# A fp32 cross-attention block: loads, biases and the written-out order at both ends of the kernel

## The chip, the cores and the metric

The kernel runs on one core of a Trainium2 chip. Everything is fp32. The metric is the device time of one execution in microseconds (us): 1021.24 us before the change, median of 3 runs (1021.12 to 1022.81). A core has five engines with an instruction stream each: TensorE (PE: matrix products and 128x128 transposes, with its weight loads shown apart as PEld), VectorE (DVE), ScalarE (ACT), GpSimd (POOL) and SyncE (SP), which here only issues DMAs. They wait for one another by semaphores.

## The reference

The block normalises x and the context, modulates both by a scale and a shift that come from a condition vector, and lets 1024 rows of x attend to 64 rows of context in 16 heads. There are 16 batches and 512 features.

```python
def _ada_ln(x, c, W_ss, b_ss):
    mu = jnp.mean(x, axis=-1, keepdims=True)
    var = jnp.mean((x - mu) ** 2, axis=-1, keepdims=True)
    h = (x - mu) / jnp.sqrt(var + EPS)
    ss = jax.nn.silu(c) @ W_ss + b_ss
    scale, bias = jnp.split(ss, 2, axis=-1)
    return (1.0 + scale)[:, None, :] * h + bias[:, None, :]

B, Lq, H = (16, 1024, 512); Lkv = 64; nh = 16; dh = 32
xq = _ada_ln(x_q, t_vec, Wss_q, bss_q)
xkv = _ada_ln(x_kv, t_vec, Wss_kv, bss_kv)
q = (xq @ Wq + bq).reshape(B, Lq, nh, dh)
kv = (xkv @ Wkv + bkv).reshape(B, Lkv, 2, nh, dh)
k = kv[:, :, 0]
v = kv[:, :, 1]
scores = jnp.einsum('bqhd,bkhd->bhqk', q, k) / jnp.sqrt(jnp.float32(dh))
attn = jax.nn.softmax(scores, axis=-1)
out = jnp.einsum('bhqk,bkhd->bqhd', attn, v).reshape(B, Lq, H)
return x_q + (out @ Wp + bp)
```

## The kernel before, in words

The 16 x 1024 rows of x are cut into 32 blocks of 512 rows (NB = 32, two blocks a batch). The context is two groups, "A" (batches 0 to 7) and "B" (8 to 15), of 512 rows each. Every instruction stands in a hand-written program: `manual_schedule()` keeps the order of the program as the order of each engine's queue, so a call that is moved in the text moves its instructions past others on each engine that it uses, and past DMAs on SyncE's queue.

Stages of one block i, by the names that the text calls:

- `load_x(i)` (L106) brings 1 MB, `q_stats` (L327) and `q_scale` (L334) make mean and reciprocal deviation, `hidden` (L345) normalises. `turn` (L367) transposes 32x32 squares on VectorE into the tile `ht` (one buffer), and `move` (L388) brings them to the other partitions by 16 DMAs; `scale_features` (L449) modulates the result. Context group "A" and "B" go by TensorE transposes instead (`turned_features`, L399), then `modulated` (L413) on VectorE and ScalarE; block 0 by `turned_products` (L430) and `turned_scaled` (L440).
- A 512x512x512 product is seven half-size products instead of eight (`seven`, L526): `context_product` (k and v of a group), `query_product` (q of a block), `product` (L932, the projection). Each is 8 records of 128x256. They need sums of operands: `column_sums` (weights, L467), `feature_sums` (L484), `row_sums` (L920), `weight_sums` (L882), nearly all on GpSimd. `context_out`, `query_out`, `query_added` and `added` (L959) take the results from PSUM. v goes to a staging tile and from there by `value_move` (L631), 8 DMAs a half, to V_A or V_B. Below, k1 or v3 is product 1 of k, or 3 of v; p11 is projection product 1 of block 1, z2 product 2 of the last block.
- `score_products(i, z)` (L656) for the two halves z of the 64 keys, `maximum` and `copied` (L679, L688) for each pair of banks, `maxima` (L714) spreads the maximum, `subtract` (L720, GpSimd, 4.55 us a half), `weights` (L726, exponentials on ScalarE), `total` (L758, GpSimd) and `row_total` (L765, VectorE) sum them. The tile of `total(i)` is one that the scores of block i+1 are copied into. `inverse_rows` (L779) takes reciprocals and brings them through DRAM (`ltd`, then `vr`), `spread_rows` (L790) spreads them, `mix` (L815) multiplies the weights by V, and `divided` (L798) divides into the tile `ot`.
- `load_residual` brings x again, `residual` (L357) adds the projection's bias on GpSimd for block 29, `biased` (L907) copies it into PSUM for the others, and `added` adds and stores.

The way in (L985 to L1407) sets up the modulation, runs both context groups and blocks 0 to 2, all ordered by hand. The loop `for i in range(3, NB - 2)` (L1409 to L1481) then does, for block i, the scores, and around them the projection of blocks i-2 and i-1 and the queries of block i+1. The way out (L1483 to L1577) ends blocks y = 30 and z = 31.

At the very start, 36 transposes of the identity (`warm`, L985) run on TensorE while the first loads are on their way. `load_scale_shift` (L139) brings the weights of the scale and shift in two parts j of two 512-KB DMAs; `scale_shift_rows` (L253) multiplies the condition by one part, `scale_shift_taken` (L271) copies the rows from PSUM, `scale_shift` (L275) transposes them and adds the biases. The biases come as a 24x128 tile by four small DMAs from GpSimd (`load_biases`, L153), and one transpose turns them (`biases`, L236).

What sets the order of DMAs is SyncE's queue. Tiles come from pools with few buffers (x: 2, `ht`: 1, the staging tile of v: 1, shared with the weight sums), so a load or a turn can wait until a former user is done.

Of the kernel before, what the change touches and what calls it, by code (L numbers as in the profile page):

```python
# [9 lines left out]
F32 = mybir.dt.float32  # L10
AF = mybir.ActivationFunctionType
ALU = mybir.AluOpType
# [8 lines left out]
def cross_attention_block(  # L21
# [117 lines left out]
    def load_scale_shift(name, w, j):  # L139
        pool, tag = SS_HOMES[name, j]  # L140
        t = pool.tile([P, NC, H], F32, tag=tag, name=f"wss_{name}_{j}")
        for h in range(2):
            at = h * H + j * (H // 2)
            nc.sync.dma_start(
                t[:, :, h * (H // 2) : (h + 1) * (H // 2)],
                w[:, at : at + H // 2].rearrange("(c p) o -> p c o", p=P),
            )
# [59 lines left out]
    ident = const.tile([P, P], F32, name="ident")  # L207
    make_identity(nc, ident)
    load_biases()
# [7 lines left out]
    WARM = 36  # L217
# [18 lines left out]
    def biases():  # L236
        pb = bank("pb", 1)
        nc.tensor.transpose(pb[:, :NBR], brow, ident[:NBR, :NBR])
        nc.vector.tensor_copy(bias_t, pb[:, :NBR])
        ones = bias_t[:, : 4 * NC].rearrange("p (n h c) -> p n h c", n=2, h=2)[:, :, 0, :]  # L240
        nc.vector.tensor_scalar_add(ones, ones, 1.0)
# [673 lines left out]
    s1_tiles, s2_tiles = {}, {}  # L915
# [4 lines left out]
    def row_sums(i, n):  # L920
# [6 lines left out]
        else:  # L927
            s2_tiles[i] = opool.tile([P, HC, HT], F32, tag="s2", name=f"s2_{i}")
            tt(s2_tiles[i], half_rows(i, 1, 1), s1_tiles[i], ALU.subtract)  # L929
            tt(half_rows(i, 0, 1), half_rows(i, 0, 1), s2_tiles[i], ALU.subtract)  # L930

    def product(i, n):  # L932
# [5 lines left out]
            4: (lambda: half_rows(i, 0, 1), lambda: half_weights(1, 1)),  # L938
# [48 lines left out]
    load_x("B")  # L987
    q_stats("A", (0,))
    q_stats("A", (1,))
    column_sums("k", w_k_sb, w_k_sums, (2,))  # L990
    first_scale(0)
    hidden("A", (0,))
    biases()
    scale_shift_rows("kv", 0)
    hidden("A", (1,))
    scale_shift_taken("kv", 0)
    turned_features("A", 0)
    scale_shift("kv", 2 * NC, 0)
    modulated("A", 0, 0, nc.vector)
    column_sums("k", w_k_sb, w_k_sums, (0,))  # L1000
    column_sums("k", w_k_sb, w_k_sums, (1,))
    q_stats("A", (2,))
    turned_features("A", 1)
    modulated("A", 0, 0, nc.scalar)
    load_query_weights()
    q_stats("A", (3,))
    column_sums("v", w_v_sb, wv_sums, (2,))
    column_sums("v", w_v_sb, wv_sums, (0,))
    first_scale(1)
    context_product("A", "k", 1)  # L1010
    hidden("A", (3,))
    scale_shift_rows("kv", 1)
    turned_features("A", 3)
    hidden("A", (2,))
    scale_shift_taken("kv", 1)
    scale_shift("kv", 2 * NC, 1)
    context_out("A", "k", 1)
    turned_features("A", 2)
    modulated("A", 0, 1, nc.scalar)
    modulated("A", 1, 1, nc.vector)  # L1020
    modulated("A", 1, 0, nc.scalar)
    modulated("A", 1, 0, nc.vector)
    context_product("A", "v", 1)
    modulated("A", 0, 1, nc.vector)
    context_product("A", "k", 2)
    context_out("A", "v", 1)
    modulated("A", 1, 1, nc.scalar)
    feature_sums("A", nc.vector, (0,))
    context_product("A", "v", 2)
    context_out("A", "k", 2)  # L1030
    context_product("A", "k", 7)
    column_sums("v", w_v_sb, wv_sums, (1,))
    feature_sums("A", nc.vector, (1,))
    column_sums("k", w_k_sb, w_k_sums, (3,))
    context_out("A", "v", 2)
    column_sums("v", w_v_sb, wv_sums, (3,))
    feature_sums("A", nc.vector, (2,))
    load_x(1)
    q_stats(0, (0,))
    q_stats(0, (1,))  # L1040
    q_stats(0, (2,))
    context_product("A", "v", 7)
    q_stats(0, (3,))
    context_product("A", "v", 6)
    q_scale(0)
    hidden(0, (2,))
    scale_shift_rows("q", 0)
    context_out("A", "v", 6)
    hidden(0, (0,))
    hidden(0, (1,))  # L1050
    hidden(0, (3,))
    scale_shift_rows("q", 1)
    context_out("A", "k", 7)
    scale_shift_taken("q", 0, 2)
    context_product("A", "k", 6)
    scale_shift("q", 0, 0, 2)
    turned_products()
    q_stats("B", (0,))
    context_out("A", "v", 7)
    q_stats("B", (3,))  # L1060
    turned_scaled(1)
    context_out("A", "k", 6)
    q_stats("B", (1,))
    column_sums("q", w_q_sb, w_q_sums, (2,))
    turned_scaled(2)
    context_product("A", "v", 5)
    q_stats("B", (2,))
    column_sums("q", w_q_sb, w_q_sums, (0,))
    q_scale("B")
    turned_scaled(3)  # L1070
    turned_scaled(0)
    hidden("B", (0,))
    hidden("B", (1,))
    context_out("A", "v", 5)
    context_product("A", "k", 5)
    context_out("A", "k", 5)
    context_product("A", "v", 3)
    hidden("B", (3,))
    feature_sums("A", nc.vector, (3,))
    context_product("A", "k", 3)  # L1080
    context_out("A", "v", 3)
    turned_features("B", 0)
    feature_sums(0, nc.gpsimd, (0,))
    feature_sums(0, nc.gpsimd, (1,))
    q_stats(1, (0,))
    turned_features("B", 1)
    q_stats(1, (3,))
    feature_sums(0, nc.gpsimd, (2,))
    turned_features("B", 3)
    q_stats(1, (2,))  # L1090
    context_out("A", "k", 3)
    context_product("A", "k", 4)
    hidden("B", (2,))
    modulated("B", 1, 1, nc.scalar)
    column_sums("q", w_q_sb, w_q_sums, (1,))
    q_stats(1, (1,))
    turned_features("B", 2)
    modulated("B", 0, 0, nc.scalar)
    query_product(0, 1)
    modulated("B", 0, 0, nc.vector)  # L1100
    q_scale(1)
    load_x(2)
    modulated("B", 1, 1, nc.vector)
    feature_sums(0, nc.gpsimd, (3,))
    modulated("B", 0, 1, nc.scalar)
    context_out("A", "k", 4)
    value_move("A", 0)
    hidden(1, (0,))
    query_seed(0)
    hidden(1, (1,))  # L1110
    modulated("B", 0, 1, nc.vector)
    feature_sums("B", nc.gpsimd, (0,))
    feature_sums("B", nc.gpsimd, (1,))
    context_product("B", "k", 1)
    hidden(1, (2,))
    load_x(3)
    column_sums("q", w_q_sb, w_q_sums, (3,))
    turn(1, (0,))
    modulated("B", 1, 0, nc.vector)
    context_product("A", "v", 4)  # L1120
    hidden(1, (3,))
    turn(1, (1,))
    query_product(0, 6)
    context_out("A", "v", 4)
    load_projection_bias()
    turn(1, (2,))
    turn(1, (3,))
    move(1, two=True)
    feature_sums("B", nc.gpsimd, (2,))
    q_stats(2, (0,))  # L1130
    modulated("B", 1, 0, nc.scalar)
    q_stats(2, (2,))
    context_out("B", "k", 1)
    query_product(0, 2)
    context_product("B", "k", 2)
    q_stats(2, (3,))
    query_out(0, 2)
    query_out(0, 6)
    context_out("B", "k", 2)
    query_product(0, 7)  # L1140
# [477 lines left out]
```

## Time and profile before

| | |
|---|---|
| median of 3 runs | 1021.24 us |
| the profiled execution: its own time | 1021.5 us |
| its span | 1019.7 us |
| mean granted TensorE clock | 0.999 |
| busy: TensorE, VectorE, GpSimd, ScalarE | 99%, 85%, 80%, 63% |
| way in: setup up to the first product of block 0 | 9.8 to 46.3 us |
| scores of block 0, 1, 2 (first half of keys) | 68.8, 93.8, 121.7 us |
| first projection product of block 1 | 145.7 us |
| way out: scores of block 30 | 943.3 us |
| last product begins | 1013.9 us |

Times in views of the trace count from the start of the span. A row of the timeline gives start, length, engine, line, operation, the tile written and the tiles read, shapes and the number of merged instructions; in square brackets stands how long the engine had been idle and what ended that. The matrix records are counted twice a call, since an fp32 call makes two. PE's, DVE's, ACT's and POOL's rows are work; SP's are issues of DMAs, whose data land later. Busy shares are averages over stages.

### The profile page before, as it was taken

The numbers are of one execution on the slowest core, as the hardware profiler recorded it, in microseconds if no ns is written. First come the engines' busy times: TensorE is split into PE (matmuls) and PEld (weight loads), VectorE is DVE, ScalarE is ACT, GpSimd is POOL, SyncE is SP. The second block draws the span as 40 slices with busy tenths as digits, with TensorE's granted clock in tenths as the row PEclk, the third lists the DMA queues.
The fourth block names the chain that finished last, engine by engine and source line by source line (L and its number), as shares of the span: only waits on it lengthen the run. The fifth ranks groups of instructions, "written<-read, shape, count | busy, mean of one in ns | idle before, by whom it ended". The sixth has DMA issues, their size and how long they took to land.

```text
span 1019.7 us, 21267 instructions
## 1 busy us (share of the span) xinstructions
PE 1006.6 (99%) x8101; PEld 767.5 (75%) x8101; DVE 862.8 (85%) x1181; ACT 638.3 (63%) x1025; POOL 811.4 (80%) x522
## 2 busy tenths in 40 slices
PE   8999999999999999999999999999999999999998
PEld 6887777777777777787777777877777777777746
DVE  6777888888898888888988888889888888876794
ACT  3777756666666666666666666667666666665530
POOL 3658898887988888889888888898888888987861
PEclk9999999999999999999999999999999999999999
DMA  9565544444445444444554444444544444335122
GB/s 314 194 177 160 148 155 134 138 144 156 156 157 167 147 130 144 127 156 148 162 167 128 127 158 133 154 155 160 167 134 127 123 155 156 117 121 167 45 86 86
DMA packets 112165, 149.82 MB, mean 147 GB/s; under 512 B 34072, under 2 KB 45360, under 8 KB 112064
## 3 DMA queue, kind: packets, MB, share of 16 engines
q1 hardware_dynamic: 111680, 147.94, 45.4%
q8 instruction: 64, 1.05, 0.4%
q0 software_dynamic: 384, 0.54, 0.2%
q14 instruction: 37, 0.30, 0.1%
HBM read 79.21 MB, written 34.60 MB: 112 GB/s over the span
## 4 chain that ended last, share of the span: by engine, by line
PE 74%; POOL 3%; DVE 3%; SPq 2%; DMA 2%; ACT 2%; issue 1%; DVEq 0%; POOLq 0%; ACTq 0%
PE pp L950 32%; PE pq L544 31%; PE ps L663 6%; PE po L831 5%; SPq L394 2%; POOL s L722 1%; DMA x<-in_x_dram 1%; ACT s L728 1%; POOL xt_sums L503 1%; DVE m L680 1%; DVE mb L709 0%; DVE l L733 0%; DMA xt<-ht 0%; ACT xt L452 0%; ACT qt L583 0%
## 5 line engine op out<-in xcount | busy, mean ns | idle before, releaser
L722 POOL TENSOR_TENSOR s<-s,mb 128x2048 f32<-128x2048 f32 x64 | 290.3, 4562 | 128.2 <-DVE mb L709 128.2
L689 ACT COPY s<-ps 128x1024 f32<-128x1024 f32 x128 | 129.5, 1013 | 106.9 <-DVE m L680 63.0
L680 DVE TRANSPOSE_TENSOR_REDUCE m<-ps 128x32 f32<-128x1024 f32 x128 | 151.3, 1217 | 32.6 <-PE ps L663 32.6
L950 PE MATMUL pp<-w_p_sb,ot 128*128 128x256 f32 x744 | 171.3, 379 | 1.4 <-DVE ot L811 0.9
L974 DVE TENSOR_TENSOR r<-pp,r 128x512 f32<-128x512 f32 x210 | 136.6, 671 | 34.3 <-PE pp L950 29.1
L950 PEld LDWEIGHTS pp<-w_p_sb,ot 128*128 128x128 f32 x744 | 141.1, 190 | 22.1 <-ACT qt L583 1.3
L583 ACT ACTIVATE qt<-pq,bias_t 128x256 f32<-128x256 f32 x256 | 105.8, 465 | 76.6 <-PE pq L544 76.4
L728 ACT ACTIVATE s<-s 128x2048 f32<-128x2048 f32 x64 | 122.4, 1912 | 40.6 <-POOL s L722 40.6
L762 POOL TENSOR_TENSOR sum<-s,s 128x2048 f32<-128x2048 f32 x31 | 140.8, 4543 | 4.3 <-ACT s L728 4.3
L950 PEld LDWEIGHTS pp<-WT,s 128*128 128x128 f32 x496 | 89.4, 189 | 58.2 <-issue 28.5
L950 PE MATMUL pp<-WT,s 128*128 128x256 f32 x496 | 123.2, 391 | 0.2 <-POOL s L929 0.2
L544 PE MATMUL pq<-xt_sums,w_q_sums 128*128 128x256 f32 x512 | 123.3, 384 | 0.0
L544 PE MATMUL pq<-xt,w_q_sb 128*128 128x256 f32 x512 | 121.5, 380 | 0.0
L544 PEld LDWEIGHTS pq<-xt_sums,w_q_sums 128*128 128x128 f32 x512 | 95.0, 190 | 34.5 <-issue 22.6
L544 PE MATMUL pq<-xt,w_q_sums 128*128 128x256 f32 x512 | 120.9, 379 | 0.0
L950 PE MATMUL pp<-WT,ot 128*128 128x256 f32 x496 | 117.5, 380 | 0.7 <-POOL ot L926 0.6
L544 PEld LDWEIGHTS pq<-xt,w_q_sb 128*128 128x128 f32 x512 | 96.8, 190 | 17.1 <-issue 2.5
L544 PEld LDWEIGHTS pq<-xt,w_q_sums 128*128 128x128 f32 x512 | 97.3, 190 | 13.2
L950 PEld LDWEIGHTS pp<-WT,ot 128*128 128x128 f32 x496 | 93.9, 190 | 15.1 <-POOL ot L926 1.0
L452 ACT ACTIVATE xt<-xt,ss_q 128x512 f32<-128x512 f32 x124 | 94.2, 809 | 8.5 <-DMA ltd<-lt 5.6
L341 ACT ACTIVATE x<-x,rstdq 128x512 f32<-128x512 f32 x128 | 97.3, 809 | 2.1 <-POOL rstdq L316 2.1
L503 POOL TENSOR_TENSOR xt_sums<-xt 128x512 f32<-128x512 f32 x64 | 81.7, 1277 | 10.4 <-ACT xt L452 7.5
(173 smaller groups left out, 1489.7 us busy)
## 6 DMA issues: line engine op xcount, KB each, us to landing
x<-in_x_dram SPq DMA_DIRECT2D x32, 1024.0 KB, 5.7
r<-in_x_dram SPq DMA_DIRECT2D x32, 1024.0 KB, 5.1
xt<-ht SPq DMA_DIRECT2D x488, 64.0 KB, 2.0
out_dram<-r SPq DMA_DIRECT2D x60, 512.0 KB, 3.7
wss_kv<-in_L_xcond_Wss_kv_dram SPq DMA_DIRECT2D x4, 512.0 KB, 8.0
wss_q<-in_L_xcond_Wss_q_dram SPq DMA_DIRECT2D x4, 512.0 KB, 10.4
vr<-ltd SPq DMA_DIRECT2D x128, 8.0 KB, 1.6
out_dram<-r SPq DMA_DIRECT2D x7, 256.0 KB, 2.1
```

What stands on the lines that cost most here:

```text
L341: nc.scalar.activation(dst, src, AF.Identity, bias=rstd[:, 1, j : j + 1], scale=rstd[:, 0, j : j + 1])
L452: nc.scalar.activation(xt[:, :, c, :], xt[:, :, c, :], AF.Identity, scale=ss["q"][:, c, b : b + 1], bias=ss["q"][:, NC + c, b : b + 1],)
L503: eng.tensor_tensor(dst, a, b, ALU.subtract)
L544: nc.tensor.matmul(out_, lhsT=lhsT, rhs=rhs, start=new and m == 0 and c == 0, stop=c == HC - 1, skip_group_check=True,)
L583: nc.scalar.activation(dst, src, AF.Identity, bias=bq_t[:, o : o + 1])
L680: nc.vector.tensor_reduce(m_tiles[i][:, z, 2 * e : 2 * e + 2, :], s_banks[i, z][e].rearrange("p r (j a) -> p r j a", a=32), AX.X, ALU.max, ...
L689: nc.scalar.copy(s_tiles[i, z][:, 2 * e : 2 * e + 2, :], s_banks[i, z][e])
L722: eng.tensor_tensor(s_tiles[i, z], s_tiles[i, z], mb_tiles[i], ALU.subtract)
L728: nc.scalar.activation(p, p, AF.Exp, scale=SCALE)
L762: nc.gpsimd.tensor_tensor(t, s_tiles[i, 0], s_tiles[i, 1], ALU.add)
L950: nc.tensor.matmul(acc[k][:, t * HO : (t + 1) * HO], lhsT=rows[:, c, t * P : (t + 1) * P], rhs=cols[:, c, :], start=n == 2 and t == 0 and ...
L974: nc.vector.tensor_add(r, a, r)
```

## The change: loads, biases, way in and way out

The changed kernel does five things; the loop's text is the same.

1. Part 0 of the context's scale and shift weights comes in four DMAs of 128 features (256 KB) instead of two of 512 KB.
2. The biases come by SyncE in two parts: the 8 rows of the context's scale and shift first, the other 16 later, each with a transpose of its own.
3. The other loads are no longer all issued at the top: they stand between the steps. `WARM` is 34 instead of 36, and nine transposes of the identity (`keep_busy`) stand between the setup's steps.
4. The steps of the way in stand in a new order: both row products of the context's modulation and all four transposes of group "A" come before its first product, and the calls of groups "A", "B" and blocks 0 to 2 are mixed anew.
5. In the way out the query products of the last block come earlier, `residual(y - 1)` moves from its head to behind `mix(y - 1)`, `mix(z)` moves up, the products of y and z have another order, and the sum s4 of the last block goes into a tile of its own.

```diff
     def load_scale_shift(name, w, j):
         pool, tag = SS_HOMES[name, j]
         t = pool.tile([P, NC, H], F32, tag=tag, name=f"wss_{name}_{j}")
+        half = H // 2
+        if (name, j) == ("kv", 0):
+            rows = w.rearrange("(c p) (h o) -> p c h o", p=P, h=2)
+            for c in range(NC):
+                nc.sync.dma_start(
+                    t[:, c, :].rearrange("p (h o) -> p h o", h=2), rows[:, c, :, :half]
+                )
+        else:
...
-    brow = early_tile(NBR, P)
-    def load_biases():
+    brow = [early_tile(2 * NC, P), early_tile(NBR - 2 * NC, P)]
+    BIASES = (((b_ss_kv, 2 * NC),), ((b_ss_q, 2 * NC), (b_q, NC), (b_kv[0:H], NC)))
+    def load_biases(k):
         at = 0
-        for src, n in ((b_ss_q, 2 * NC), (b_ss_kv, 2 * NC), (b_q, NC), (b_kv[0:H], NC)):
-            nc.gpsimd.dma_start(brow[at : at + n, :], src.rearrange("(r f) -> r f", f=P))
+        for src, n in BIASES[k]:
+            nc.sync.dma_start(brow[k][at : at + n, :], src.rearrange("(r f) -> r f", f=P))
             at += n
...
     load_first(0)
     load_first(1)
     load_scale_shift("kv", w_ss_kv, 0)
-    load_context_weights(0, 0)
-    load_first(2)
-    load_first(3)
-    load_scale_shift("kv", w_ss_kv, 1)
-    load_context_weights(1, 0)
-    load_context_weights(0, 1)
-    load_context_weights(1, 1)
-    load_value_bias()
-    load_x(0)
-    load_scale_shift("q", w_ss_q, 0)
-    load_scale_shift("q", w_ss_q, 1)
...
-    WARM = 36
+    WARM = 34
...
+            s4 = half_rows(i, 0, 1)
+            if i == NB - 1:
+                s4 = rpool.tile([P, HPC * TB], F32, tag="spread", name="s4")
+                s4 = s4[:, : HC * HT].rearrange("p (c n) -> p c n", c=HC)
+            s4_tiles[i] = s4
+            tt(s4, half_rows(i, 0, 1), s2_tiles[i], ALU.subtract)
...
-    load_x("B")
+    idle = bank("idle", 0)
+
+    def keep_busy(n):
+        for _ in range(n):
+            nc.tensor.transpose(idle[:, :P], ident, ident)
+
```

The way in of the changed kernel, from behind the warm-up to its first product (lines that do not bear on the setup are left out):

```python
    q_stats("A", (0,))
    q_stats("A", (1,))
    load_first(2)
    first_scale(0)
    load_biases(0)
    hidden("A", (0,))
    load_first(3)
    load_scale_shift("kv", w_ss_kv, 1)
    scale_shift_rows("kv", 0)
    keep_busy(2)
    biases(0)
    hidden("A", (1,))
    q_stats("A", (2,))
    load_context_weights(0, 0)
    scale_shift_taken("kv", 0)
    load_biases(1)
    load_context_weights(1, 0)
    q_stats("A", (3,))
    turned_features("A", 0)
    turned_features("A", 1)
    load_context_weights(0, 1)
    load_context_weights(1, 1)
    keep_busy(3)
    scale_shift("kv", 2 * NC, 0)
    modulated("A", 0, 0, nc.vector)
    first_scale(1)
    keep_busy(4)
    scale_shift_rows("kv", 1)
    modulated("A", 0, 0, nc.scalar)
    ...
    turned_features("A", 2)
    ...
    turned_features("A", 3)
    ...
    scale_shift("kv", 2 * NC, 1)
    ...
    biases(1)
    context_product("A", "k", 1)
```

Further on, between the scores of block 1 and the first projection product of block 1 (changed kernel, the calls that the prediction speaks of):

```python
    total(0)
    ...
    move(3)
    ...
    score_products(1, 0)
    row_total(0)
    copied(1, 0, 0)
    maximum(1, 0, 1)
    context_product("B", "v", 5)
    maximum(1, 0, 0)
    inverse_rows(0)
    context_product("B", "v", 7)
    ...
    context_out("B", "v", 7)
    copied(1, 0, 1)
    score_products(1, 1)
    maximum(1, 1, 0)
    maximum(1, 1, 1)
    maxima(1)
    query_product(2, 1)
    ...
    context_out("B", "v", 5)
    ...
    mix(0)
    q_stats(5, (0,))
    turn(4, (0,))
    turn(4, (1,))
    context_product("B", "v", 3)
    context_out("B", "v", 3)
    ...
    value_move("B", 0)
    ...
    value_move("B", 1)
    ...
    load_x(6)
    ...
    move(4)
    ...
    inverse_rows(1)
    ...
    spread_rows(1)
    added(0, 4)
    turn(5, (1,))
    added(0, 3)
    ...
    divided(1)
    ...
    product(1, 1)
```

`value_move("A", 1)` stands in the changed kernel behind `move(2)` and before `load_x(5)` and `move(3)`; before, it stood ahead of `load_x(4)` and `move(2)`.

The way out from the last block's scores on, changed kernel:

```python
    scores(z, 0, crossed=True)
    total(y)
    mix(y - 1, apart=False, ks=(2, 3, 1, 0))
    residual(y - 1)
    divided(y - 1)
    scores(z, 1)
    row_total(y)
    project(y - 1, 0)
    inverse_rows(y)
    maxima(z)
    project(y - 1, 1)
    project(y - 1, 2, later=True)
    subtract(z)
    load_residual(y)
    spread_rows(y)
    projected(y - 1, 2)
    weights(z, 0)
    mix(y)
    weights(z, 1)
    project(y - 1, 3, later=True)
    divided(y)
    row_sums(y, 0)
    product(y, 1)
    sums(z, 0)
    product(y, 2)
    added(y, 1)
    sums(z, 1)
    halves_total(z)
    mix(z)
    inverse_rows(z)
    projected(y - 1, 3)
    row_sums(y, 1)
    product(y, 6)
    added(y, 2)
    product(y, 7)
    added(y, 6)
    product(y, 5)
    added(y, 7)
    biased(z, 2)
    product(y, 4)
    added(y, 5)
    product(y, 3)
    spread_rows(z)
    divided(z)
    row_sums(z, 0)
    product(z, 1)
    biased(z, 3)
    added(y, 3)
    added(y, 4)
    row_sums(z, 1)
    product(z, 2)
    added(z, 1)
    ...
```

More of the change, by code (lines that the diff above doesn't have):

```diff
@@ L1032, in cross_attention_block @@
[L1032 to L1038, printed above, removed]
+    hidden("A", (3,))
+    turned_features("A", 2)
+    column_sums("k", w_k_sb, w_k_sums, (0,))
+    turned_features("A", 3)
+    column_sums("v", w_v_sb, wv_sums, (0,))
+    modulated("A", 0, 1, nc.scalar)
+    scale_shift("kv", 2 * NC, 1)
@@ L1065, in cross_attention_block @@
[L1065 to L1082, printed above, removed]
@@ L1119, in cross_attention_block @@
+    query_seed(0)
     modulated("B", 1, 0, nc.vector)
     context_product("A", "v", 4)
-    hidden(1, (3,))
-    turn(1, (1,))
-    query_product(0, 6)
[L1124 to L1130, printed above, removed]
+    context_out("A", "v", 3)
+    hidden(1, (0,))
+    modulated("B", 0, 0, nc.vector)
+    hidden(1, (1,))
+    turn(1, (0,))
+    load_x(3)
+    hidden(1, (2,))
@@ L1172, in cross_attention_block @@
+    turn(2, (3,))
+    copied(0, 0, 1)
+    scale_features(1, (2,))
+    maximum(0, 0, 1)
+    context_product("B", "k", 4)
+    copied(0, 0, 0)
+    load_x(4)
+    q_scale(3)
+    score_products(0, 1)
+    scale_features(1, (3,))
+    query_product(1, 1)
+    context_out("B", "k", 5)
+    context_out("B", "k", 4)
+    context_product("B", "k", 3)
+    maximum(0, 1, 0)
+    maximum(0, 1, 1)
+    maxima(0)
+    move(2)
+    hidden(3, (0,))
+    query_seed(1)
+    context_out("B", "k", 3)
     feature_sums(1, nc.gpsimd, (0,))
-    context_product("B", "k", 5)
@@ L1226, in cross_attention_block @@
[L1226 to L1238 removed]
+    context_out("B", "v", 6)
+    query_out(1, 3)
+    scale_features(2, (1,))
+    score_products(1, 0)
+    row_total(0)
+    copied(1, 0, 0)
+    feature_sums(2, nc.gpsimd, (0,))
+    maximum(1, 0, 1)
+    context_product("B", "v", 5)
```

678 lines of the change are left out of this document (343 added, 335 removed).

## The prediction

> **What bounds the kernel now.** I read the page first, for the engine that is never idle, and then the busy time by stretch, to see in which stage that engine waits.
>
> ```profile
> span 1019.7 us, 21267 instructions
> ...
> PE 1006.6 (99%) x8101; PEld 767.5 (75%) x8101; DVE 862.8 (85%) x1181; ACT 638.3 (63%) x1025; POOL 811.4 (80%) x522
> ```
>
> ```profile
> 9.70:35.90 26.20, 24.14 (x231) 19.03 (x231) 19.63 (x53) 11.87 (x33) 12.38 (x13) 1.00 0.96 324
> 145.70:943.30 797.60, 797.41 (x6522) 609.83 (x6522) 697.06 (x909) 519.22 (x807) 666.85 (x406) 1.00 0.46 146
> 943.30:1014.00 70.70, 68.56 (x546) 45.88 (x546) 52.41 (x56) 21.83 (x25) 43.66 (x22) 1.00 0.19 67
> ```
>
> In the second table the columns are the stretch, its length, then the busy time of TensorE, its weight loads, VectorE, ScalarE and GpSimd, the granted clock, the DMA share and GB/s. TensorE is the bound. In the loop (145.7 to 943.3) it is busy 797.41 of 797.60 us, and the loop's text is the same in both kernels: nothing is to be had there. The change can only win TensorE's idle time outside it: 2.06 us in the first stretch (26.20 less 24.14), 2.14 us in the way out (70.70 less 68.56), and what the middle of the way in holds. So the question is how many of these few microseconds go, and whether they are paid again further on. A difference of 0.2%, 2.04 us, is about what a measurement of this kernel can tell from no change.
>
> **The change part by part: setup.** These are TensorE's instructions in the first 36 us (start, length, line, operation, count, and in brackets the wait before it), and the DMA queue's order.
>
> ```profile
> 3.13 6.59 PE L986 MATMUL warm<-ident 128*128 128x128 f32 x36
> ...
> 9.95 1.08 PE L260 MATMUL ps_kv<-wss_kv,early 128*32 128x128 f32 x32
> ...
> 13.00 2.15 PE L544 MATMUL pk_A<-xk_A,w_k_sb 128*128 128x256 f32 x8 [0.79 <-ACT xk_A L426]
> 15.09 1.60 PE L260 MATMUL ps_kv<-wss_kv,early 128*32 128x128 f32 x32
> ...
> 18.23 1.89 PE L544 MATMUL pv_A<-w_v_sb,xk_A 128*128 128x256 f32 x8
> ...
> 29.78 1.71 PE L260 MATMUL ss_q<-wss_q,early 128*32 128x128 f32 x56
> ...
> 34.31 1.72 PE L435 MATMUL pxt<-ident,x 128*128 128x128 f32 x14 [0.42 <-DVE ss_q L288]
> ```
>
> ```profile
> 3.15 0.51 SPq L167 DMA_DIRECT2D w_k_sb<-in_L_xcond_Wkv_dram  x1
> ```
>
> First weights in four loads: the last byte comes through the same pipe, so the last quarter lands no earlier than the second half did; only three quarters of the row products can run before it. The rows start right behind the warm-up (9.95 against 3.13 + 6.59 = 9.72, with one small transpose between). Two dummies fewer are 2 x 6.59/36 = 0.37 us. Bounds: 0 (the last quarter decides) to 1.08 us (all rows hidden); I take 0.5 for the first row. It matters little, since k1 no longer follows it directly.
>
> In a sentence apart: the Trainium skill, "DMA: Bandwidth & Descriptors", section "Rules for kernel authors", asks for at least 1 MiB in one DMA, and so speaks against quarter loads of 256 KB; the trace moves 324 GB/s over the first stretch with loads of 256 to 1024 KB, and I estimate that by the page's fixed cost of about 2 us a DMA, paid in a row, two more loads would put the first rows 4 us later, while by the trace, where issued loads overlap, they cost their issue (0.51 us each) and nothing behind that.
>
> Biases on the SyncE queue: two or three more issues of about 0.5 us (the row at 3.15) stand in front of later loads. They hide as long as the pipe is full, which it is (share 0.96). Without that cover they cost some 1.5 us once. The split adds a transpose and three short VectorE operations in gaps; I set them at nothing (bounds 0 to 0.5).
>
> Order of the setup: k1 stood at 13.00, between the two row groups; now both groups, all transposes and nine dummies come first. The second row group took 1.60 instead of 1.08 us: its second half waited till about 15.6. In the changed queue the 512-KB half of w_k (issued at 3.15) stands behind that load, which gains 0.52 MB / 324 GB/s = 1.6 us, so it lands near 14.0. From the end of that wait to v1 at 18.23 passed 2.6 us; so k1 comes between 14.0 + 2.6 = 16.6 and 17.8, since all four context tiles must now be modulated before; I take 17.2. It is 4.2 us later, but then nothing stands between the products. With 1.72 us for a product (1012.20 to 1013.92, quoted below), nine of them are 15.5, the 64 records of the query rows 1.71 x 64/56 = 1.95, the sixteen transposes of block 0 1.72 x 16/14 + 0.42 = 2.4, small ones 0.2: the end of that group comes at 17.2 + 20.0 = 37.2, with one product more than the 36.03 of before (34.31 + 1.72) had. So 35.5 against 36.0: a gain of 0.5, bounds -0.1 and +1.1.
>
> **The middle.** Here is what stands between the scores of block 1 and the first projection product of block 1, whose time fixes the loop's start, as the same four products follow it in both kernels.
>
> ```profile
> 96.28 2.27 DVE L767 TRANSPOSE_TENSOR_REDUCE lt<-sum 128x64 f32<-128x2048 f32 x1
> ...
> 100.90 2.38 DVE L680 TRANSPOSE_TENSOR_REDUCE m<-ps 128x32 f32<-128x1024 f32 x2 [0.18 <-PE ps L663]
> ...
> 106.65 0.66 DVE L624 TENSOR_TENSOR stage_B<-pv_B,b_v_sb 128x512 f32<-128x512 f32 x1
> ```
>
> ```profile
> 99.70 2.17 PE L663 MATMUL ps<-qt,K_A 32*32 32x512 f32 x32 [1.13 <-ACT s L689]
> ```
>
> ```profile
> 107.34 13.28 SPq L636 DMA_DIRECT2D V_B<-stage_B  x16
> ...
> 121.36 11.84 SPq L394 DMA_DIRECT2D xt<-ht  x16
> ```
>
> ```profile
> 139.73 2.31 DVE L793 STREAM_TRANSPOSE vb<-vr 128x2048 f32<-128x2048 f32 x1 [0.31 <-DMA vr<-ltd]
> ...
> 143.14 1.28 DVE L372 STREAM_TRANSPOSE ht<-x 128x512 f32<-128x512 f32 x2
> 144.34 2.32 DVE L811 TENSOR_TENSOR ot<-po,vb 128x1024 f32<-128x1024 f32 x2
> ```
>
> ```profile
> 145.68 1.53 PE L950 MATMUL pp<-w_p_sb,ot 128*128 128x256 f32 x6 [0.90 <-DVE ot L811]
> ```
>
> The second scores waited 1.13 us for copies that could not write before the row total (96.28 + 2.27) had read their tile. The row total is now put ahead of both maxima, its sum ahead of other GpSimd work: I take that wait as gone. So TensorE is about 0.5 + 1.1 us ahead at 100.
>
> But p11 waits for the division, that for the spread, that for rows through DRAM, and those stand on SyncE behind 32 transfers, V_B (13.28 us) and move(4) (11.84 us), which start only when v3 is staged (106.65 + 0.66 = 107.31, then 107.34). That queue is the lock. In the changed order v3 stands behind more of VectorE: the maxima start at 100.90 - 1.6 = 99.3; from there to v3 passed 5.75 us (106.65 - 100.90); v5's addition (0.66, as v3's) and two turns of block 4 (1.28) are put in front. That is 99.3 + 5.75 + 1.94 = 107.0, with some drains 107.3: V_B starts at 107.6 to 108.0, 0.3 to 0.7 later in spite of the earlier scores. Behind the spread one turn fewer (0.64) stands before the division. So p11 comes at 145.7 + 0.5 - 0.64: 0.2 us earlier, and TensorE, ahead by 1.6, waits for it longer than the 0.90 of now. Bounds: -1.6 (the lock moves as early as the scores do) and +0.6. What the head won is mostly lost again here.
>
> **The way out.** TensorE, ScalarE, VectorE and GpSimd there:
>
> ```profile
> 990.83 1.99 PE L950 MATMUL pp<-WT,ot 128*128 128x256 f32 x8 [0.60 <-POOL ot L926]
> ...
> 994.97 1.97 PE L950 MATMUL pp<-w_p_sb,ot 128*128 128x256 f32 x8 [0.42 <-DVE r L974]
> ...
> 998.59 2.35 PE L831 MATMUL po<-s,V_B 32*32 32x512 f32 x64
> ...
> 1002.99 3.72 PE L950 MATMUL pp<-w_p_sb,ot 128*128 128x256 f32 x16
> ...
> 1012.20 1.89 PE L950 MATMUL pp<-w_p_sb,ot 128*128 128x256 f32 x8
> 1013.92 1.89 PE L950 MATMUL pp<-WT,ot 128*128 128x256 f32 x8
> ```
>
> ```profile
> 988.59 0.59 ACT L913 COPY pp<-b_p_sb 128x512 f32<-128x512 f32 x1 [2.95 <-DVE r L871]
> ```
>
> ```profile
> 993.72 0.55 DVE L782 RECIPROCAL lt<-lt 128x64 f32<-128x64 f32 x1
> ...
> 999.30 2.30 DVE L793 STREAM_TRANSPOSE vb<-vr 128x2048 f32<-128x2048 f32 x1
> 1001.71 2.35 DVE L811 TENSOR_TENSOR ot<-po,vb 128x1024 f32<-128x1024 f32 x2
> ```
>
> ```profile
> 949.50 4.97 POOL L359 TENSOR_TENSOR r<-r,b_p_sb 128x512 f32<-128x512 f32 x4
> ...
> 979.13 9.07 POOL L722 TENSOR_TENSOR s<-s,mb 128x2048 f32<-128x2048 f32 x2 [8.64 <-DVE mb L709]
> ```
>
> mix(z), 2.35 us at 998.59, moves up behind the first two projection products and fills the 0.60 and 0.42 us waits: 1.0 at most. That counts only if the last block's products can start earlier. Its division hangs on the reciprocal at 993.72; the bias copy (0.59) ahead of the last exponentials goes, and with it about 0.75 us of that chain: division at 1001.0 to 1003.3. Then the adds of p3 and p4 stand on VectorE, 0.65 each: z2 cannot take its bank before 1003.3 + 1.3 = 1004.6. Before, z1 and z2 are the sixteen records at 1002.99, so z2 started at 1002.99 + 1.72 = 1004.7. So z1 gains 0.75, z2 nothing, and those behind it the short wait for row sums, which the earlier division removes. I take 0.4 (bounds 1.0 and -0.4, if an add slips one more place). The last block's s4 in its own tile costs no instruction. The residual (4.97 us on GpSimd) moves into the 8.64 us in which it waits before 979.13: nothing; without that cover it would push the last chain by up to 5.
>
> **Sum:** -0.2 (all ahead of the loop) - 0.4 (way out) = -0.6 on the profiled 1021.5, 1020.9. That run lies 0.26 above the median of 1021.24, so the forecast for the median is 1020.6.
>
> **The rivals.** *A lock that opens.* If v3 is staged as early as the scores allow, the 1.6 us won by then reach the loop, and the way out gives its 1.0: 1021.24 - 2.6 = 1018.6; with the rest of the idle time of the first stretch, up to 1 us more, 1017.6. For it: p11 hangs on one VectorE order, where half a microsecond decides. Against: the two turns and v5 are written ahead of v3.
>
> *The queue of moves shuts later* (the slower one). V_A's second half, 5.18 us, now stands behind move(2) and ahead of move(3).
>
> ```profile
> 62.66 5.18 SPq L636 DMA_DIRECT2D V_A<-stage_A  x8
> ...
> 72.38 11.98 SPq L394 DMA_DIRECT2D xt<-ht  x16
> ...
> 92.20 10.02 SPq L394 DMA_DIRECT2D xt<-ht  x16
> ```
>
> ```profile
> xt<-ht SPq DMA_DIRECT2D x488, 64.0 KB, 2.0
> ```
>
> Block 4's turns write the tile that move(3) reads, and v3 is behind them. If move(3) starts 5.18 later than now, it is issued by 107.4 and landed at 109.4; turns 1.28, v3 0.66: V_B at 111.4, 4.0 late, less 0.64 and 0.4: 1021.24 + 3.0 = 1024.2. It decides from a landing past 106 on. Against it: move(2) is over at 84.4, V_A then at 89.6, and move(3) would be issued from there on, ahead of its 92.20 of now, landing at 104.
>
> *It doesn't do what it says:* the last quarter lands with the old second half, the waits change place, 1021.2.
>
> *A cold TensorE.* The view of line 986 shows the weight loads of the warm-up, minimum, median and maximum:
>
> ```profile
> L986 PEld LDWEIGHTS warm<-ident x36: 139/230/230, 3.1 to 9.3; 128*128 128x128 f32 x36
> ```
>
> More than half of them ran at 230 ns, at least 18 x 6.59/36 = 3.3 us, before the rate of 139. If the thin work up to 17.2 lets that state come back, the same 3.3 us at 139/230 of the rate lose 3.3 x 0.4 = 1.3 us: 1021.24 - 0.6 + 1.3 = 1021.9. The nine dummies speak against it. The Trainium skill, "TensorE: Matmul & The Clock Gate", Part 1, has this rule: the clock halves after an idle window of about 3.4 us; by its figure the loss would be an estimated 1.7 us, and the trace agrees as to the start (230 to 139), while the granted clock stays at 1.00 in its rows.
>
> **How the numbers follow.** Forecast 0.42, lock open 0.32, moves late 0.17, no effect 0.04, cold 0.05. The second is faster by over 0.2%, the third slower by over 0.2%, the others (0.51) within. The forecast's own range, from the bounds above, is 1019.2 to 1022.2. The range for 8 in 10 takes in the open lock down to 1017.4 and the late moves up to 1023.4.
>
> **What would show it.** Right: first rows near 9.5, k1 near 17, products without gaps to 37, no wait before the second scores of block 1, V_B issued from about 107.8, p11 near 145.5 with a wait of over 2 us ahead of it; in the way out mix(z) near 990, division near 1001, the last product near 1013.4 less the head's 0.2. Wrong: V_B before 106.5 or p11 before 144.5 (lock open), move(3) after 95 (moves late), products of over 2.3 us around 17 to 21 (cold), or a wait of GpSimd's subtraction of the last block past 979.

## The result and the profile after

The changed kernel takes 1019.43 us (median of 8, 1018.54 to 1021.49), the kernel before, in the same session, 1022.06 us (median of 8, 1020.81 to 1023.13). The ratio is 0.9977, interval 0.9967 to 0.9986: about 2.35 us faster (1.4 to 3.4). The forecast was 0.6 us faster, which it called no measurable change; its range for 8 in 10 (1017.4 to 1023.4) held the time.

The one profiled execution of the changed kernel took 1021.49 us, the slowest of its eight, and its span, 1019.7 us, equals that of before. So the spans say nothing; the stages do. The loop has the same text in both kernels, but in these two profiles it lasts 790.7 us after (153.09 to 943.80) and 788.8 us before (154.49 to 943.29). The view of the waits from 144 to 943 us shows what one execution of it can meet (engine, line, what it waited for, total, times, longest):

```profile
ACT xt L455 <- DMA xt<-ht: 3.8, 4, 1.9
...
PE pq L547 <- ACT qt L586: 1.4, 2, 0.7
```

Twice TensorE stood 0.7 us: a query product waited for ScalarE, and ScalarE had waited up to 1.9 us for a landing of the moves. Over all fourteen profiles of this study the loop lasts between 788.2 and 790.7 us. What the change does must therefore be read ahead of 154 us and behind 943 us.

TensorE in the setup and at the first scores of block 0, changed kernel (same columns as in the prediction):

```profile
9.36 1.08 PE L263 MATMUL ps_kv<-wss_kv,early 128*32 128x128 f32 x32
...
14.21 1.07 PE L263 MATMUL ps_kv<-wss_kv,early 128*32 128x128 f32 x28 [0.68 <-DMA wss_kv<-in_L_xcond_Wss_kv_dram]
15.78 1.09 PE L410 MATMUL pxk_A<-ident,x_A 128*128 128x128 f32 x8 [0.51 <-DVE x_A L354]
...
17.07 2.00 PE L547 MATMUL pk_A<-xk_A,w_k_sb 128*128 128x256 f32 x8
...
24.31 2.00 PE L547 MATMUL pk_A<-xk_sums_A,w_k_sums 128*128 128x256 f32 x8
26.62 1.96 PE L547 MATMUL pk_A<-xk_sums_A,w_k_sums 128*128 128x256 f32 x8 [0.32 <-DVE xk_sums_A L506]
...
36.30 2.17 PE L438 MATMUL pxt<-ident,x 128*128 128x128 f32 x16
```

The second row weights land near 14.2 (forecast 14.0) and k1 starts at 17.07 (forecast 17.2). From there to the end of block 0's transposes at 38.31 (36.30 + 2.01, the next product's start) pass 21.24 us, where the forecast summed 20.0. With nine products done instead of eight that is 38.31 - 1.72 = 36.6, against 35.87 before (the start of the product behind block 0's transposes): in these two profiles the setup is 0.7 us behind, not 0.5 ahead.

The middle, TensorE, then SyncE, then VectorE:

```profile
67.78 1.14 PE L666 MATMUL ps<-qt,K_A 32*32 32x512 f32 x32
...
93.40 1.61 PE L666 MATMUL ps<-qt,K_A 32*32 32x512 f32 x32 [0.37 <-ACT qt L586]
...
99.02 1.30 PE L666 MATMUL ps<-qt,K_A 32*32 32x512 f32 x32 [0.36 <-ACT s L692]
...
100.25 1.99 PE L547 MATMUL pq<-xt,w_q_sb 128*128 128x256 f32 x8
...
123.65 1.14 PE L666 MATMUL ps<-qt,K_A 32*32 32x512 f32 x32
...
128.37 1.14 PE L666 MATMUL ps<-qt,K_A 32*32 32x512 f32 x32
...
133.09 2.35 PE L834 MATMUL po<-s,V_A 32*32 32x512 f32 x64
...
144.11 1.89 PE L958 MATMUL pp<-w_p_sb,ot 128*128 128x256 f32 x8
...
153.09 1.14 PE L666 MATMUL ps<-qt,K_A 32*32 32x512 f32 x32
```

```profile
108.93 10.37 SPq L639 DMA_DIRECT2D V_B<-stage_B  x16
```

```profile
138.63 2.27 DVE L796 STREAM_TRANSPOSE vb<-vr 128x2048 f32<-128x2048 f32 x1
...
142.59 2.34 DVE L814 TENSOR_TENSOR ot<-po,vb 128x1024 f32<-128x1024 f32 x2
```

The first projection product of block 1 (p11) has no wait any more and comes at 144.11 instead of 145.68, although V_B begins 1.6 us later than before. From the first scores of block 0 to the first of block 3, TensorE needs 153.09 - 67.78 = 85.31 us, with one product more in it (at 67.78 one fewer had been done): 83.6 against 85.7 before (154.49 - 68.80). Two more profiles with the old way in, among the experiments below, have 85.26, so this gain is 1.7 to 2.1 us. TensorE before:

```profile
68.80 1.14 PE L663 MATMUL ps<-qt,K_A 32*32 32x512 f32 x32
...
101.80 1.99 PE L544 MATMUL pv_B<-w_v_sb,xk_sums_B 128*128 128x256 f32 x8
...
121.74 1.14 PE L663 MATMUL ps<-qt,K_A 32*32 32x512 f32 x32
...
126.99 1.30 PE L663 MATMUL ps<-qt,K_A 32*32 32x512 f32 x32
...
131.87 2.35 PE L831 MATMUL po<-s,V_A 32*32 32x512 f32 x64
...
154.49 1.14 PE L663 MATMUL ps<-qt,K_A 32*32 32x512 f32 x32
```

The gain has three places. Up to the end of block 1's scores it is 0.5 us (100.25 - 67.78 = 32.47 against 101.80 - 68.80 = 33.00). From there to block 2's scores the new order has two more products, and with 1.73 us for each there is no difference. From block 2's scores to the mix of block 1 it is 0.7 us (9.44 against 10.13, with as many products). From that mix to block 3's scores, past p11, the new order has one product fewer: 20.00 + 1.73 = 21.73 us stand against 22.62 here and 22.2 in the two other profiles of the old way in, a gain of 0.5 to 0.9.

The way out, TensorE and VectorE:

```profile
943.80 1.14 PE L666 MATMUL ps<-qt,K_B 32*32 32x512 f32 x32
...
990.66 2.35 PE L834 MATMUL po<-s,V_B 32*32 32x512 f32 x64
...
1002.74 1.97 PE L958 MATMUL pp<-w_p_sb,ot 128*128 128x256 f32 x8 [0.90 <-DVE ot L814]
1005.07 1.97 PE L958 MATMUL pp<-w_p_sb,ot 128*128 128x256 f32 x8 [0.36 <-DVE r L982]
...
1013.78 1.89 PE L958 MATMUL pp<-WT,ot 128*128 128x256 f32 x8
```

```profile
1001.37 2.35 DVE L814 TENSOR_TENSOR ot<-po,vb 128x1024 f32<-128x1024 f32 x2
```

From the scores of block 30 to the last product: 69.98 us, before 70.63 (1013.92 - 943.29). The waits of 0.60 and 0.42 us are gone and two new ones, 0.90 (for the division) and 0.36 (for an add), stand ahead of z1 and z2. Together: 1.40 us ahead of the loop and 0.65 behind it, 2.05 of the 2.35 measured.

### The profile page after: what moved, and what is told of

Its sections match the earlier page's. It is cut to its first block, busy times and chain, and to the rows that moved or that the text cites. A ratio compares the mean times of both kernels' runs of the same rounds, so it can differ in the third digit from the quotient of the medians.

```text
span 1019.7 us, 21289 instructions
## 1 busy us (share of the span) xinstructions
PE 1007.1 (99%) x8109; PEld 770.6 (76%) x8109; DVE 864.3 (85%) x1184; ACT 637.6 (63%) x1025; POOL 808.1 (79%) x518
## 4 chain that ended last, share of the span: by engine, by line
PE 88%; DVE 3%; POOL 3%; DMA 2%; ACT 1%; SPq 1%; issue 1%; DVEq 0%; POOLq 0%; ACTq 0%
PE pp L958 35%; PE pq L547 35%; PE po L834 7%; PE ps L666 6%; POOL s L725 2%; PE pp L861 1%; PE pk_A L547 1%; PE pv_A L547 1%; PE pk_B L547 1%; SPq L397 1%; ACT s L731 1%; DVE m L683 1%; DMA wss_kv<-in_L_xcond_Wss_kv_dram 1%; DMA x<-in_x_dram 1%; DVE mb L712 0%
## 5 line engine op out<-in xcount | busy, mean ns | idle before, releaser
L301 DVE BATCH_NORM_STATS2 bs<-x 128x6 f32<-128x512 f32 x128 | 87.0, 680 | 0.3 <-DMA x<-in_x_dram 0.3
```

The source lines that it names most:

```text
L301: nc.vector.bn_stats(bs, r)
```

## The experiments

The theories: *queue* (SyncE's V_B, which before stood 2.9 us in its middle for v4's addition, held p11), *VectorE's order*, and *TensorE's order*. Times are compared with the kernel before; positions come from one profile of each kernel.

**Each end alone.** The kernel before with the new way out, and the changed kernel with the old way out.

> The kernel before with the changed way out alone (with the last block's s4 tile). If the two ends add up, the way in and the loop are as before: first projection product of block 1 (p11) at 145.7 us, and from the first scores of block 30 to the begin of the last product 70.0 instead of 70.6 us, so the time falls by about 0.5 us (ratio 0.9995). A rival says that the changed way out needs the changed way in to pay: then no difference in that stretch.

> The changed kernel with the way out of before. If the two ends add up: p11 at 144.1 instead of 145.7, the stretch of the way out 70.6 us as before, time lower by about 1.6 us (ratio 0.9984). The rival, that the loop gives the head's gain back (in the one profile of the changed kernel the scores of block 30 came at 943.8, later than before), says that the ratio is 1.000 within its interval.

New way out alone: ratio 0.9989 (0.9981 to 0.9998), its stretch 1012.79 - 942.81 = 69.98 us. New way in alone: 0.9982 (0.9973 to 0.9991), p11 at 144.01, way out 1012.67 - 942.03 = 70.64. The two ends add up to 0.9971, the whole change has 0.9977 (0.9967 to 0.9986). The rivals, that one needs the other or that the loop eats the gain, fall.

**The queue: its pause closed in the old kernel, and v4 put back late in the new one.** Before, SyncE's transfers to V_B stand still in their middle till VectorE has added v4 (SyncE, then VectorE):

```profile
110.97 1.90 SPq L636 DMA_DIRECT2D V_B<-stage_B  x3
...
115.53 1.87 SPq L636 DMA_DIRECT2D V_B<-stage_B  x3
```

```profile
114.84 0.66 DVE L629 TENSOR_TENSOR stage_B<-pv_B,stage_B 128x512 f32<-128x512 f32 x1
```

From 112.87 to 115.53 nothing is issued; the view of the queue's waits counts 2.9 us.

```diff
     spread_rows(0)
+    context_out("B", "v", 4)
     turn(4, (0,))
...
     product(0, 1)
-    context_out("B", "v", 4)
     query_added(2, 5)
```

> The kernel before, with one VectorE instruction moved: the addition of v4 into the staging tile stands right behind the spread of block 0 instead of behind its division. Queue theory (SyncE stood 2.9 us in the middle of V_B's sixteen transfers for this addition): V_B is issued without a gap in about 10.4 us instead of 13.3, the spread of block 1 comes up to 2.5 us earlier, p11 loses its wait of 0.9 and starts at 144.8, time lower by 0.9 us (ratio 0.9991). Rival (the gain is TensorE's own new order and the scores' shorter waits): V_B's gap closes, p11 moves by less than 0.2.

> The changed kernel, with the addition of v4 put back behind the division and the first projection product of block 0, as before. Queue theory: V_B's second half waits until about 115.4, the sixteen end near 120.6 instead of 119.3, p11 has a wait again and comes 0.8 to 1.2 us later than 144.1, time about 1 us over the changed kernel's (ratio to before near 0.9987 instead of 0.9977). Rival (TensorE's order): p11 stays within 0.2 of 144.1.

With v4 early in the kernel before, SyncE and TensorE:

```profile
107.38 11.22 SPq L636 DMA_DIRECT2D V_B<-stage_B  x16
```

```profile
145.28 1.97 PE L950 MATMUL pp<-w_p_sb,ot 128*128 128x256 f32 x8 [0.47 <-DVE ot L811]
```

The gap in V_B is closed (11.22 instead of 13.28 us), but p11 still waits 0.47; the ratio is 0.9994 (0.9985 to 1.0004). The first experiment's way in, unaltered from before and with 12.44 us for V_B, also shows 0.47 there, and both need 85.26 us from block 0's scores to block 3's: closing the gap won nothing. Of the 0.90 in the profile of before, some 0.4 go with the late landing ahead of its spread (the wait of 0.31 at 139.73 in the prediction's rows), which the other two profiles do not have. In the changed kernel with v4 late (reverse edit), the addition still came at 113.66, as the division ahead of it was early, and V_B took 10.94 instead of 10.37 us. The pause was hardly there again, so this run does not test the queue. Its p11 stood at 143.72 with the first scores at 67.38: 76.34 us between them, as in the changed kernel (144.11 - 67.78 = 76.33). The ratio is 0.9972 (0.9960 to 0.9984). The expected 0.8 to 1.2 us did not come. That the queue is not what the change gained rests on the run in the old kernel.

**Three moves of VectorE's new order, in the old kernel.**

```diff
-    maximum(1, 0, 1)
     row_total(0)
+    maximum(1, 0, 1)
...
     spread_rows(0)
+    context_out("B", "v", 4)
...
-    q_stats(6, (2,))
     turn(5, (0,))
...
-    turn(5, (2,))
     divided(1)
+    q_stats(6, (2,))
+    turn(5, (2,))
```

> The kernel before with three moves on VectorE alone in the middle of the way in: the row total of block 0 ahead of both maxima, v4's addition right behind the spread of block 0, and one statistic and one turn put behind the division of block 1. If VectorE's order is what sets the middle (the scores of block 1 and the first projection product of block 1, p11), the scores' 1.13 us wait falls below 0.4, p11's 0.90 goes, p11 starts near 144.0 and the time falls by about 1.6 us (ratio 0.9984, as the whole changed way in). Rival: the new order on TensorE is needed as well, and p11 stays later than 144.9 (ratio 0.9992 or more).

```profile
100.53 2.17 PE L663 MATMUL ps<-qt,K_A 32*32 32x512 f32 x32 [1.53 <-ACT s L689]
...
145.43 1.89 PE L950 MATMUL pp<-w_p_sb,ot 128*128 128x256 f32 x8
```

The row total ahead of both maxima made the scores' wait longer, 1.53 instead of 1.13 us, since the maxima, and the copies behind them, now came after it. In the changed kernel the first copy stands ahead of the maxima too (`copied(1, 0, 0)` in the listing ahead of the prediction), and the copies start at 96.89, 0.1 us behind the row total; here they started at 99.46. p11's wait went: from the mix of block 1 to block 3's scores TensorE took 154.29 - 132.69 = 21.60 us, against 22.2 with v4 early alone, so the statistic and the turn behind the division are worth 0.6 us there. The row total lost 0.4 (102.62 - 69.22 = 33.40 to the end of block 1's scores, against 33.00). Ratio 0.9998 (0.9988 to 1.0007): the three moves together gain nothing that the times show. They are not VectorE's whole new order, which was not run alone.

**TensorE's order around the scores of block 2.** First the old kernel with one query product moved ahead of them (and, not shown in the cut, the statistic and the turn put behind the division as above), then the changed kernel with the same product put back.

```diff
+    query_product(3, 1)
     score_products(2, 0)
...
-    query_product(3, 1)
```

> The kernel before with two small moves: the first query product of block 3 ahead of the scores of block 2 instead of between their halves, and one statistic and one turn put behind the division of block 1. In the kernel before, the products and scores from the first half of block 2's scores to the mix of block 1 take 0.9 us more than their records need. If TensorE's order around these scores is the cause, that falls to 0.2, p11 has no wait, the time from the first scores of block 0 to those of block 3 falls from 85.3 to 85.7 us to about 84.0, and the time by 1.3 us (ratio 0.9987). Rival (VectorE alone, as in the run with three moves): 85.1 us, ratio 0.9998.

> The changed kernel with that one product put back between the halves of block 2's scores. TensorE's order: the extra of 0.7 to 0.9 us around these scores is back, and the time from the first scores of block 0 to those of block 3 rises from 85.31 to about 86.1 us. Rival: VectorE's order in the changed kernel covers it, and it stays within 0.2 of 85.31.

Old kernel, product ahead:

```profile
124.09 1.14 PE L663 MATMUL ps<-qt,K_A 32*32 32x512 f32 x32
125.16 1.99 PE L950 MATMUL pp<-WT,ot 128*128 128x256 f32 x8
127.63 1.25 PE L663 MATMUL ps<-qt,K_A 32*32 32x512 f32 x32 [0.48 <-ACT s L689]
```

Changed kernel, product back:

```profile
122.60 2.05 PE L666 MATMUL ps<-qt,K_A 32*32 32x512 f32 x32
...
129.96 1.28 PE L666 MATMUL ps<-qt,K_A 32*32 32x512 f32 x32
```

In the old kernel one product alone is left between the two halves, and the second half waits 0.48 us for its banks: block 0 to block 3 takes 154.06 - 68.96 = 85.1 us, as the rival said; ratio 0.9993 (0.9984 to 1.0001). The two moves on VectorE again give 21.60 us behind the mix of block 1 (154.06 - 132.46) and no wait at p11; the product cost 0.4 up to that mix (132.46 - 68.96 = 63.50 us, in the first experiment's old way in 63.07). In the changed kernel the product put back costs: the first half stretches from 1.14 to 2.05 us, and 154.82 - 68.48 = 86.34 us stand against 85.31, 1.0 us more (expected 0.8); its one time is 1022.10 us. So in these profiles the same move is worth 1 us in the new order and costs 0.4 in the old one, where a second product between the halves is then missing. What a place is worth depends on the order around it.

**The setup.** The old loads, biases and order up to block 0's transposes, and the new order behind them.

> The loads, biases and order of the kernel before up to the transposes of block 0, and the changed kernel's order from there on (v5, which the changed kernel has ahead of them, follows them). In the changed kernel the first scores of block 0 came at 67.78 with one product fewer done than before at 68.80: its setup is 0.7 us behind. If so, they come here at about 67.1, p11 near 143.4, ratio 0.9970. Rival: the later chain over VectorE and SyncE holds p11 at 144.1, and the ratio is that of the changed kernel, 0.9977.

The first scores of block 0 came at 67.75, not 67.1, p11 at 144.19; ratio 0.9967 (0.9954 to 0.9979), not to be told from the changed kernel's. The ratio is near the expected 0.9970 without the positions that it was worked out from. The setup's 0.7 us could not be won this way: the first row weights were late there (a wait of 0.33 us on their load), and other small waits followed.

**Three parts of the setup in the changed kernel**: without the nine dummy transposes (twice), with two loads instead of four, with the biases issued by GpSimd.

> The changed kernel without its nine dummy transposes in the setup. If they only lie in waits (for the second row weights, which landed near 14.2), the first scores of block 0 stay at 67.8 within 0.3 us. The cold-clock rival expects the products behind 17 us at up to 2.8 instead of 1.73 us each for 3.3 us, and the scores 1.3 us later.

> The same kernel as the run without dummies, timed. There the granted clock was 0.71 from 17 to 21 us, and the first scores of block 0 came 0.8 us later. If the thin work ahead of the first product lets the clock fall in most executions, the profile shows a clock below 0.9 again in that stretch, scores at 68.4 or later, and the ratio is 0.998 to 0.9985 (changed kernel 0.9977). If it was chance, clock 1.00, scores at 67.8, ratio 0.9977.

> The changed kernel with the first scale and shift weights in two loads of 512 KB again. The second row weights' load sets the first product, so the first scores of block 0 stay at 67.8 within 0.3 us, whether the first rows start at 9.4 as now or up to 0.6 us later. If quarter loads matter, the scores come later by the delay of the first rows.

> The changed kernel with its bias loads issued by GpSimd, at the same places and in the same two parts. If it does not matter who issues them, the first scores of block 0 stay at 67.8 within 0.3 us. If their issues on SyncE had delayed the loads behind them, the second row weights come up to 1.5 us earlier (near 13) and the scores with them.

Without dummies the first scores came at 68.60 and, in the second run, at 68.44. The four profiles with the changed setup as it is have 67.38 to 68.48, 67.8 in the mean: 0.7 later, but not clear of their spread. The ratio of the second run is 0.9991 (0.9981 to 1.0001), where the changed kernel has 0.9977 (0.9967 to 0.9986). Busy time by stretch, second run without dummies (columns as in the prediction's table: the granted clock stands behind the five engines):

```profile
11.00:14.00 3.00, 1.70 (x13) 1.07 (x13) 2.82 (x11) 0.72 (x3) 0.00 (x0) 1.00 1.09 360
14.00:17.00 3.00, 2.25 (x34) 1.99 (x35) 1.82 (x9) 1.87 (x5) 0.00 (x0) 0.78 1.10 348
17.00:21.00 4.00, 4.00 (x17) 3.27 (x16) 2.93 (x14) 3.17 (x11) 1.54 (x2) 0.74 1.07 365
```

and its transposes of "A":

```profile
15.82 1.97 PE L410 MATMUL pxk_A<-ident,x_A 128*128 128x128 f32 x8 [0.70 <-DVE x_A L354]
```

The changed kernel:

```profile
11.00:14.00 3.00, 2.42 (x20) 1.75 (x20) 2.86 (x11) 0.76 (x3) 0.00 (x0) 1.00 1.10 362
14.00:17.00 3.00, 2.29 (x38) 1.86 (x38) 1.78 (x8) 1.92 (x6) 0.00 (x0) 1.00 1.11 349
17.00:21.00 4.00, 4.00 (x19) 3.54 (x20) 3.85 (x17) 4.00 (x14) 0.92 (x1) 1.00 1.06 362
```

The clock fell to 0.78 and 0.74, and the eight transposes took 1.97 instead of 1.09 us. Both runs show it, so it was not chance. k1 started at 18.26 and 18.14, against 16.65 to 17.57 in the four; some of that was won back, since k6 did not wait then. The two ratios' intervals overlap, so no cost in time is shown.

Two loads: the first rows start at 9.95 instead of 9.36, the scores at 67.88. With loads of 128 features the rows start between 8.94 and 9.86 in the four profiles, so one profile with two loads shows no gain from the smaller ones; by the scores it is 0.1 us at most. Biases by GpSimd: the scores came at 67.03, 0.75 us earlier than in the changed kernel's profile and outside the expected 0.3, but only 0.35 ahead of the earliest of the four. Its rows show why only in part:

```profile
24.18 3.64 PE L547 MATMUL pk_A<-xk_sums_A,w_k_sums 128*128 128x256 f32 x16
```

k1 started at 17.17, as with SyncE, but k6 followed k7 without the wait for VectorE's feature sums that stood ahead of it at 26.62. That wait varies among profiles of this way in (0.15 with two loads, 0.55 with the product put back), and there is one profile with GpSimd's biases. Whether the issuer matters stays open.

## Why the prediction was right and wrong

- *The sum:* the range held, in part by luck. Ahead of the loop the forecast had 0.2 us and the two profiles show 1.40, made of a setup that lost 0.7 where it was to win 0.5 and a middle that won some 2 where most was to be lost.
- *The loop decides nothing, and only its two ends can win:* right. The two ends alone give 0.9989 and 0.9982.
- *Setup, 0.5 us ahead:* wrong in sign. The loads and k1 came as worked out (14.2 and 17.07), but the nine products with what lies between them took 21.24 instead of 20.0 us. The term that was too small is the one for products "without gaps": k6 waited 0.58 us past its due time for feature sums, v1 to k7 took 0.23 more than a product's 1.72, and a product next to another kind of record took 0.1 to 0.2 more each time (k1, behind small transposes, 1.83 to its successor). The sixteen transposes took 0.4 less than summed. In five profiles with the old setup the first scores come at 68.8 to 69.2, in four with the new one at 67.4 to 68.5, which is 69.1 to 70.2 with the missing product added.
- *The scores of block 1 no longer wait:* half right. The 1.13 us fell to 0.36, but 0.37 appeared ahead of their first half, for the query's bias copy, which the forecast did not have; 0.5 us was won by their end, not 1.1. The reason was too short as well: with the row total ahead of both maxima and the copies still behind them, the wait grew to 1.53. What the copies of the changed kernel have besides is their place ahead of the maxima; that was not run alone.
- *The lock at p11, "0.2 us earlier":* the step that failed. The forecast held that SyncE's 32 transfers start when v3 is staged and fix p11. V_B did start later, at 108.93 and even later than the forecast's 107.6 to 108.0, and p11 still came 1.57 us earlier, with no wait. A row of sixteen merged issues, 13.28 us, was read as a time of issue; it held a pause of 2.9 us for v4's addition, and the new order has 10.37. But the queue did not hold p11 either: with the pause closed in the old kernel 0.47 us of wait is left, as without that. What p11 waited for is VectorE's work ahead of the division: with a statistic and a turn put behind it, the wait was gone in both runs. The forecast had the turn (0.64), and the division does stand 3.96 instead of 4.61 us behind the spread; but it had the spread 0.5 us later, with the queue, and it came 1.1 earlier (138.63 against 139.73).
- *Where the middle's 2 us come from:* the sum had no term for the scores of block 2. Before, from these to the mix of block 1 passed 0.7 us more than in the changed kernel, whose two halves start 4.72 us apart (123.65, 128.37; before 126.99 - 121.74 = 5.25) with the same two kinds of products between them. Putting one product back there costs 1.0 us. The scores of block 1 give 0.5, and p11's wait 0.5 to 0.9, which the two moves on VectorE give in the old kernel too. The first two parts were not reproduced: the queue, the row total and one product alone do not give them, and which moves they need was not separated.
- *Way out, 0.4 us earlier:* right in mechanism, small by 0.25. The division came at 1001.37, 57.57 us behind the scores of block 30 (before 58.42): 0.85 earlier, forecast 0.75; z2 was indeed held by an add (0.36), and won 0.16 where the forecast had nothing.
- *The rivals:* the time is near that of the open lock (1018.6), but not by its mechanism, as v3 was not staged early. The moves were not late: move(3) was issued from 91.38. No TensorE in the cold, as long as the dummies are there. Without them the clock fell as that rival has it; priced at 1.3 us, it cost 0.7 at the first scores in the mean of two profiles, which is not clear of the spread.

## What to carry to other kernels

A merged row of DMA issues can hide a wait: look at the first and last of them, and at what the queue waited for, before its length is used as a price. Look in the trace, too, whether an experiment's edit did to its stage what it was meant to: v4 put back late did not bring the pause back. When TensorE is the bound, sum its starts against what its records need, stage by stage; that shows waits of a few tenths that no list of longest waits shows. And where a kernel varies by 2 us between executions, compare the stages that a change touches, not two spans.

## What the runs showed of the hardware that was not expected

The granted clock fell though TensorE was never idle for long: without the dummies it was busy 1.70 of 3.00 us from 11 to 14 (second run), the longest wait in the trace there was 0.92 us (ahead of 14.05), and the clock had a mean of 0.78 from 14 to 17 and of 0.74 from 17 to 21; in steps of half a microsecond it reads 0.50 from 16.0 to 19.0, in both runs. With the dummies, 2.42 of 3.00, it stayed at 1.00; and the dummies are transposes. Thin work in one such stretch does not do it: with the product put back, TensorE was busy 1.44 of 3.00 us from 14 to 17, waited 1.56 us ahead of 16.28, and kept its clock.

```profile
14.00:17.00 3.00, 1.44 (x35) 1.18 (x26) 2.29 (x10) 2.29 (x7) 0.00 (x0) 1.00 1.11 352
17.00:21.00 4.00, 4.00 (x22) 3.42 (x21) 3.44 (x16) 3.59 (x13) 1.78 (x2) 1.00 1.05 366
```

From 11 to 17 together TensorE was busy 3.94 and 3.95 of 6.00 us in the two runs whose clock fell, and 4.34 to 4.93 in the twelve whose clock did not; where the limit lies was not measured. The Trainium skill, "TensorE: Matmul & The Clock Gate", Part 1, has the clock halved after an idle window of about 3.4 us; the trace agrees that it halves, and differs in that no such idle stretch was needed.
